# The input of a decoder's last feed-forward layer: normalisation and quantisation of three pairs of batches moved into the cross attention before it, square roots from the bits, and a quantiser in 16 bits

## The chip, the cores and the metric

The kernel runs on one core of a Trainium2 chip. A core has a TensorE (PE, with its weight loads, PEld), a VectorE (DVE), a ScalarE (ACT), a GpSimd (POOL) and a SyncE (SP), each of which works through a queue of its own in order. The metric is the device time of one execution in microseconds. Times at a place in the run are counted from the start of the profiled span.

## The reference

A decoder of three layers, each of self attention, cross attention and a feed-forward network (FFN), over 8 batches of 112 tokens with 256 values, and a context of 375 tokens with 128 values per batch. Every sublayer takes the layer-normalised `x` and is added to `x`. The change is at the end:

```python
x = x + _L3_xattn_ref(_layernorm(x, axis=-1), ctx_512, ...)   # 16 heads of 16, softmax over 375 keys
x = x + _L3_ffn_ref(_layernorm(x, axis=-1), gate_w, up_w, down_w, s_in, s_in_down)

def fake_quant_nvfp4(x, global_scale):
    xb = x.reshape(sh[:-1] + (sh[-1] // 16, 16))             # blocks of 16
    amax = jnp.max(jnp.abs(xb), axis=-1, keepdims=True)
    sc = jnp.clip(amax / 6.0 * global_scale, 0.0, 448.0)
    sc8 = sc.astype(jnp.float8_e4m3fn).astype(jnp.float32)   # scale of a block in 8 bits
    dq = sc8 / global_scale
    a = jnp.clip(jnp.abs(xb) / where(dq == 0, 1, dq), 0.0, 6.0)
    return sign(xb) * round_to(a, [0, .5, 1, 1.5, 2, 3, 4, 6]) * dq

hidden = silu(q(x) @ q(gate_w).T) * (q(x) @ q(up_w).T)       # 1024 hidden values
return q(hidden) @ q(down_w).T
```

All three weights, the input and the hidden values go through the quantiser `q`.

## The kernel before

`decoder` calls the twelve sublayers one after the other. Within most of them the inner loops stand in a `manual_schedule` region: there PE, DVE and ACT get their instructions in the order in which the code issues them. Outside such regions a scheduler decides the order on each engine from what is ready, so that the start of a sublayer can run within the end of the one before.

The names that the change touches:

- `rsqrt` (lines 410 to 422) takes variances to reciprocal roots: on DVE `va = var + eps`; on ACT a Sqrt (L415); on DVE a reciprocal (L416) and one Newton step of four operations (L418 to L421). It is called from `stats`, and this from `normalise` and `ln_T`, 35 times in the run, mostly on [112, 4] values. [...]the Sqrt takes a table load before it, and the next exponential, gelu or silu another.
- `cross` (from line 1088) is the cross attention of two layers. For each batch `b` and each group `c` of four heads it runs one step of this order: `turn` 0 and 1 (PE transposes the exponentials of one head in three pieces, DVE or ACT copies them out as `xeT`: even heads on DVE, odd ones on ACT), `key` of the next batch (c = 0, 2), `summed` (c = 1) or `divide` (c = 3) of the batch before, `turn` 2, `score` of the next step (four products into PSUM), `turn` 3, `exponent` of the next step (four maxima `xnm` on DVE, L1165; four exponentials `xe` on ACT, L1169), `value` of the next batch (PE, then the copy `xv` on DVE, L1136; c < 3), the `result` of the batch before (c = 3: projection, then the addition to `x`), and `attend` (24 products). The buffers in PSUM: `tr` two, `sc` four, `mm` and `av` one each. After the last step come the sums, a widening on POOL (`xrw`), the division (`xoT`) and the projection of the last batch.
- `quantise` (from line 1968) is the quantiser on DVE: block maxima by one reduction with absolute values (L1985), a chain on one value per block that rounds the scale to 8 bits and takes its reciprocal (L1987 to L2001), and seven operations on all values (L2004 to L2011): product with the reciprocal, clipping, exponent bits, a scaled power of two, its addition and subtraction (which rounds), and the product with the scale. All but the output are 32-bit.
- `l3_weights` quantises the three weights under the second layer's FFN, in halves of 1024 values, and transposes them.
- `l3_ffn` (from line 2060) normalises `x`, quantises it in two halves of 1024 values (four batches each), transposes each half on PE (`xqT`), and then goes over four pairs of batches: gate and up products `gu`, Silu `sg` on ACT, the product `hid` on DVE (L2104, from PSUM), `quantise` of 2048 values, transposes, a copy on ACT, the products `y` and the addition to `x` (L2121). It has no `manual_schedule`.
- `store` sends `x` out.

Of the kernel before, what the change touches and what calls it, by code (L numbers as in the profile page):

```python
# [22 lines left out]
BF16 = mybir.dt.bfloat16  # L23
AF = mybir.ActivationFunctionType
# [89 lines left out]
def _weights(inp):  # L114
# [135 lines left out]
    raw = [_fm(f("gate_w")), _fm(f("up_w")), _fm(f("down_w"))]  # L250
# [102 lines left out]
class _Kernel:  # L353
# [56 lines left out]
    def rsqrt(self, var, rows, n):  # L410

        nc, small = self.nc, self.small
        va, sd, rs, t = (self.t(small, [P, 24], tag)[:rows, :n] for tag in ("va", "sd", "rs", "nt"))
        nc.vector.tensor_scalar(va, var, EPS, None, ALU.add)
        nc.scalar.activation(sd, va, AF.Sqrt)  # L415
        nc.vector.reciprocal(rs, sd)  # L416

        nc.vector.tensor_tensor(t, rs, rs, ALU.mult)  # L418
        nc.vector.tensor_tensor(t, t, va, ALU.mult)
        nc.vector.tensor_scalar(t, t, -0.5, 1.5, ALU.mult, ALU.add)  # L420
        nc.vector.tensor_tensor(rs, rs, t, ALU.mult)  # L421
        return rs
# [666 lines left out]
    def cross(self, name, cT, qsrc, wq, wk, wv, wo, hd, scale, finish, ctx, bq=None, bk=None, bv=None):  # L1089
# [14 lines left out]
        nc, tc = self.nc, self.tc  # L1104
        acts = ctx.enter_context(tc.tile_pool(name=f"{name}_q", bufs=1))
# [135 lines left out]
        with tc.manual_schedule(engines={ET.PE, ET.DVE, ET.Activation}):  # L1241
            score(0, 0)
            exponent(0, 0)
            for n, (b, c) in enumerate(steps):
                turn(b, c, 0)
                turn(b, c, 1)
# [12 lines left out]
                if c < 3 and b + 1 < NB:  # L1259
                    value(b + 1, c)  # L1260
# [10 lines left out]
            if dense:  # L1271
                summed(NB - 1)
            divide(NB - 1)
            result(NB - 1)

# [683 lines left out]
    def l3_xattn(self):  # L1959
        w = self.w  # L1960
        with ExitStack() as ctx:
            self.cross(
                "l3x", self.ctxT, self.ln_T, w("l3x_wq", 2), w("l3x_wk"), w("l3x_wv"), w("l3x_wo", 4), 16, 0.25,
                self.add_to_x, ctx,
            )
        w.done("l3x_wo")

    def quantise(self, pool, src, dst, rows, n, gs, amax=None):
# [3 lines left out]
        nb = n // 16  # L1972

        def blocks(a):
            return a.rearrange("p (k e) -> p k e", e=16)

        def bc(a):
            return a[:, :, None].to_broadcast([rows, nb, 16])

        def sm(tag):  # L1980
            return self.t(pool, [P, nb], f"q{tag}{nb}")[:rows]

        if amax is None:
            amax = sm("m")
            nc.vector.tensor_reduce(amax, blocks(src), AX.X, ALU.max, apply_absolute_value=True)  # L1985
        sc, st, z = sm("s"), sm("t"), sm("z")
        nc.vector.tensor_scalar(sc, amax, 1.0 / 6.0, gs, ALU.mult, ALU.mult)  # L1987
        nc.vector.tensor_scalar(sc, sc, 448.0, None, ALU.min)

# [7 lines left out]
        nc.vector.tensor_tensor(sc, sc, st, ALU.subtract)  # L1997
        nc.vector.scalar_tensor_tensor(z, sc, 0.0, sc, ALU.is_equal, ALU.add)
        nc.vector.reciprocal(z, z)

        nc.vector.tensor_scalar(z, z, gs, 1.0 + 2.0**-23, ALU.mult, ALU.mult)  # L2001
        a = self.t(pool, [P, n], f"qa{n}")[:rows]
        m = self.t(pool, [P, n], f"qm{n}")[:rows]
        nc.vector.tensor_tensor(blocks(a), blocks(src), bc(z), ALU.mult)  # L2004
        nc.vector.tensor_scalar(a, a, 6.0, -6.0, ALU.min, ALU.max)

        nc.vector.tensor_scalar(m.bitcast(I32), a.bitcast(I32), 0x7F800000, None, ALU.bitwise_and)
        nc.vector.tensor_scalar(m, m, 1.0, 0.5 * big, ALU.max, ALU.mult)
        nc.vector.tensor_tensor(a, a, m, ALU.add)
        nc.vector.tensor_tensor(a, a, m, ALU.subtract)  # L2010
        nc.vector.tensor_tensor(blocks(dst), blocks(a), bc(sc), ALU.mult)  # L2011
# [146 lines left out]
```

## Time and profile before

| | us |
|---|---|
| median of three runs | 2435.77 (2435.06 to 2436.54) |
| the profiled execution | 2432.16 |
| its span | 2430.4 |
| PE busy | 2138.1 (88%) |
| DVE busy | 1434.3 (59%) |
| ACT busy | 826.8 (34%) |
| POOL busy | 215.8 (9%) |

One execution was profiled, and every duration below is from it. The execution's own time is 1.8 us above its span. A row of the profile names a line of the kernel, an engine and an operation, what is written and read (buffer numbers left out), and the shapes (partitions x elements, type). A row of the timeline starts with the time in the span and the busy time, and has in brackets how long the engine was idle before it and what ended that. Busy times are averages over stages that have different limits, so the table by stage matters more than the shares of the span.

### The profile page before, as it was taken

The page shows a single profiled execution, that of the slowest core. Times are in us where ns is not written, and L with a number is a line of the kernel's source. Part 1 is how long each engine was busy: PE and PEld are TensorE (multiplying, and loading weights), DVE is VectorE, ACT ScalarE, POOL GpSimd, SP SyncE. Part 2 cuts the span into 40 slices and gives each one's busy share as a digit, 9 for nine tenths or more (in the row PEclk, how much of TensorE's full clock was granted, in tenths as well). Part 3 has the DMA queues.
Part 4 walks back from the last instruction along what each step waited for, and adds up shares of the span by engine and source line. Part 5 has one row for each costly group of instructions (what it writes and reads, how often), then busy time and mean ns, then how long its engine had stood idle before and what let it go on. Part 6 is the DMA issues. An engine that isn't in the chain of part 4 may idle for free.

```text
span 2430.4 us, 43101 instructions
## 1 busy us (share of the span) xinstructions
PE 2138.1 (88%) x17032; PEld 1268.6 (52%) x17032; DVE 1434.3 (59%) x3810; ACT 826.8 (34%) x2220; POOL 215.8 (9%) x415
## 2 busy tenths in 40 slices
PE   6999999889899899899988859899999999899842
PEld 3444444455556566546555536466555556556622
DVE  4555556565446567553877547767740223667698
ACT  2333334453312356430111213467321111346521
POOL 0111111000011100000222331100000000100000
PEclk9999999999999999999999979999999999899966
DMA  4000000000100000100001011000111100000000
GB/s 185 2 2 2 2 20 35 29 18 18 52 1 15 18 1 2 36 26 18 35 18 35 18 28 52 17 2 19 53 35 62 41 1 1 1 1 2 2 1 15
DMA packets 10729, 55.93 MB, mean 23 GB/s; under 512 B 1833, under 2 KB 3625, under 8 KB 5792
## 3 DMA queue, kind: packets, MB, share of 16 engines
q1 hardware_dynamic: 8304, 44.57, 5.1%
q0 software_dynamic: 2080, 7.07, 0.9%
q8 instruction: 135, 2.21, 0.4%
q10 hardware_dynamic: 144, 1.54, 0.2%
q14 instruction: 66, 0.54, 0.1%
HBM read 52.23 MB, written 0.92 MB: 22 GB/s over the span
## 4 chain that ended last, share of the span: by engine, by line
PE 66%; DVE 22%; issue 5%; ACT 4%; DMA 2%; POOL 1%; DVEq 0%; ACTq 0%; POOLq 0%
PE mm L407 31%; PE tr L1178 6%; PE gu L407 6%; PE g L640 6%; PE sc L407 4%; PE av L1194 3%; PE tr L407 1%; DVE rot L1487 1%; PE av L777 1%; ACT sg L651 1%; PE av L407 1%; ACT th L662 1%; PE s L407 1%; DVE hT L666 1%; DMA cx<-in_ctx 1%
## 5 line engine op out<-in xcount | busy, mean ns | idle before, releaser
L640 PE MATMUL g<-w,hT 128*32 128x256 f32 x3552 | 237.4, 384 | 26.0 <-DVE hT L666 24.6
L1178 PEld LDWEIGHTS tr<-cst,xe 112*125 112x125 f32 x1152 | 151.5, 188 | 96.7 <-issue 37.0
L1165 DVE TENSOR_REDUCE xnm<-sc 112x1 f32<-112x375 f32 x384 | 184.3, 540 | 29.5 <-PE sc L407 28.9
L1178 PE MATMUL tr<-cst,xe 112*125 112x112 f32 x1152 | 193.1, 289 | 8.6 <-DVE xeT L1186 3.5
L407 PE MATMUL mm<-xnT,w 128*128 128x448 f32 x432 | 183.0, 559 | 19.7 <-DVE qT L1490 4.5
L407 PE MATMUL mm<-hT,w 128*128 128x448 f32 x512 | 193.0, 539 | 0.0
L640 PEld LDWEIGHTS g<-w,hT 128*32 128x32 f32 x3552 | 95.7, 109 | 167.5 <-DVE hT L666 124.6
L407 PEld LDWEIGHTS mm<-hT,w 128*128 128x128 f32 x512 | 97.1, 190 | 94.4 <-issue 94.4
L1186 DVE COPY xeT<-tr 125x336 f32<-125x336 f32 x192 | 97.3, 507 | 70.4 <-PE tr L1178 63.0
L618 PE MATMUL g<-xw,cst 128*32 128x256 f32 x1792 | 138.7, 379 | 0.0
L1184 ACT COPY xeT<-tr 125x336 f32<-125x336 f32 x192 | 85.0, 443 | 155.8 <-PE tr L1178 155.8
L407 PE MATMUL mm<-w,hT 128*112 128x256 f32 x576 | 132.6, 389 | 0.0
L407 PEld LDWEIGHTS mm<-xnT,w 128*128 128x128 f32 x432 | 77.8, 193 | 102.8 <-issue 52.6
L1169 ACT ACTIVATE xe<-sc,xnm 112x375 f32<-112x375 f32 x256 | 126.2, 581 | 9.5 <-DVE xnm L1165 9.2
L407 PE MATMUL mm<-w,oT 128*112 128x256 f32 x416 | 105.8, 405 | 24.0 <-DVE oT L1667 15.2
L407 PE MATMUL gu<-xnT,w 128*128 128x448 f32 x320 | 124.4, 544 | 1.7 <-DVE hT L1332 1.2
L407 PEld LDWEIGHTS mm<-w,hT 128*112 128x112 f32 x576 | 103.7, 182 | 27.5 <-issue 4.8
L651 ACT ACTIVATE sg<-g 128x192 f32<-128x192 f32 x224 | 73.9, 330 | 105.4 <-PE g L640 94.1
L662 ACT ACTIVATE th<-cell 128x64 f32<-128x64 f32 x224 | 57.5, 257 | 147.2 <-DVE cell L660 147.1
L407 PEld LDWEIGHTS mm<-w,oT 128*112 128x112 f32 x416 | 73.9, 186 | 54.1 <-DVE oT L1667 16.3
L664 DVE TENSOR_TENSOR h<-sg,th 128x64 f32<-128x64 f32 x224 | 50.4, 225 | 84.8 <-ACT th L662 84.8
L2046 DVE COPY wq<-tr 128x256 bf16<-128x256 bf16 (+1 forms) x12 | 4.6, 420 | 157.5 <-PE tr L2045 157.5
(398 smaller groups left out, 3673.3 us busy)
## 6 DMA issues: line engine op xcount, KB each, us to landing
w<-in_w SPq DMA_DIRECT2D x33, 1024.0 KB, 4.9
raw<-in_wq POOLq DMA_DIRECT2D x3, 1024.0 KB, 5.3
w<-in_w SPq DMA_DIRECT2D x3, 896.0 KB, 6.4
wi<-in_wint POOLq DMA_DIRECT2D x3, 768.0 KB, 5.6
w<-in_w SPq DMA_DIRECT2D x2, 768.0 KB, 4.2
ctxT<-in_ctxT ACTq DMA_DIRECT2D x1, 1500.0 KB, 8.3
cx<-in_ctx POOLq DMA_DIRECT2D x1, 1500.0 KB, 22.5
w<-in_w SPq DMA_DIRECT2D x2, 512.0 KB, 3.5
```

The lines of the kernel that those rows point to most:

```text
L407: self.nc.tensor.matmul(out, lhsT, rhs, start=i == 0, stop=i == len(pairs) - 1)
L618: nc.tensor.matmul(g[32 * j : 32 * j + 32, :], pick[:, t % 16, :], xw[:, l, t // 16, 256 * j : 256 * j + 256], start=True, stop=t == 0, sk ...
L640: nc.tensor.matmul(g[32 * j : 32 * j + 32, :], hT[l][:, c, :], whh[l][:, c, 256 * j : 256 * j + 256], start=False, stop=c == 1, skip_group ...
L651: nc.scalar.activation(sg[:, :192], g[:, :192], AF.Sigmoid)
L662: nc.scalar.activation(th, cell[l], AF.Tanh)
L664: nc.vector.tensor_tensor(h, og, th, ALU.mult)
L1165: nc.vector.tensor_reduce(nm, sc, AX.X, ALU.max, negate=True)
L1169: nc.scalar.activation(e, sc, AF.Exp, bias=nm)
L1178: nc.tensor.transpose(tp[:CH, i * S : (i + 1) * S], e[:, i * CH : (i + 1) * CH], self.ident[:S, :S])
L1184: nc.scalar.copy(eT, src)
L1186: nc.vector.tensor_copy(eT, src)
L1194: nc.tensor.matmul(avs[b][32 * j : 32 * j + 32, c * S : (c + 1) * S], values[b % 2][:CH, i, 4 * c + j, :], eTs[b, c, j][:, i, :], start=i ...
```

## The change

It has four parts.

1. `rsqrt` becomes ten operations on DVE, without ACT: a first guess from the bits of the float (shift right by one, subtract from a constant), one step of a tuned polynomial, one Newton step. `rsqrt_steps` yields within them.
2. `quantise` becomes a generator that yields after every few operations. Blocks are laid out in strides (element `e` of block `k` at `e * k_count + k`) and not side by side, so that a scale is spread over contiguous values; the weights are permuted on the host to match. The block maxima are taken of absolute values that ACT wrote (`mag`), by four maxima of halves on DVE (`block_max`); the weights keep the reduction. The quotient is cut to its upper 16 bits with the lowest bit set, and clipping, exponent bits, rounding and the last product are done in bf16.
3. The input of the last FFN goes by pairs of batches (512 values), each a generator `l3f_input` of 17 steps. `cross` calls `meanwhile(n, ps)` at places in its order; a call runs one step of the first pair whose batches are done. In the cross attention of the third layer that gives three pairs; the fourth follows in the FFN.
4. The FFN's loop gets a `manual_schedule`. While one pair is quantised the gate and up products of the next are issued between the steps, the result of a batch is issued after its half of the last product, and the additions to `x` come one pair later.

```diff
     def rsqrt(self, var, rows, n):
+        *_, rs = self.rsqrt_steps(var, rows, n)
+        return rs
+    def rsqrt_steps(self, var, rows, n):
-        nc.vector.tensor_scalar(va, var, EPS, None, ALU.add)
-        nc.scalar.activation(sd, va, AF.Sqrt)
-        nc.vector.reciprocal(rs, sd)
-        nc.vector.tensor_tensor(t, rs, rs, ALU.mult)
-        nc.vector.tensor_tensor(t, t, va, ALU.mult)
-        nc.vector.tensor_scalar(t, t, -0.5, 1.5, ALU.mult, ALU.add)
-        nc.vector.tensor_tensor(rs, rs, t, ALU.mult)
+        vec.tensor_scalar(va, var, EPS, None, ALU.add)
+        vec.tensor_scalar(r0.bitcast(I32), va.bitcast(I32), 1, None, ALU.logical_shift_right)
+        vec.tensor_scalar(r0.bitcast(I32), r0.bitcast(I32), -1.0, float(0x5F300000), ALU.mult, ALU.add)
+        yield
+        root = 0.446405130**0.5
+        vec.scalar_tensor_tensor(w, r0, root, va, ALU.mult, ALU.mult)
+        vec.tensor_tensor(w, w, r0, ALU.mult)
+        vec.scalar_tensor_tensor(p, w, -1.38883461 / root, w, ALU.add, ALU.mult)
+        yield
+        vec.scalar_tensor_tensor(p, p, 1.94247540, r0, ALU.add, ALU.mult)
+        vec.scalar_tensor_tensor(w, p, -0.5, va, ALU.mult, ALU.mult)
+        vec.tensor_tensor(w, w, p, ALU.mult)
+        vec.scalar_tensor_tensor(rs, w, 1.5, p, ALU.add, ALU.mult)
+        yield rs
...
     # cross
             for n, (b, c) in enumerate(steps):
                 turn(b, c, 0)
+                meanwhile(b - 1, ps)
                 turn(b, c, 1)
...
                     exponent(*steps[n + 1])
-                if c < 3 and b + 1 < NB:
-                    value(b + 1, c)
+                if c < 3:
+                    meanwhile(b - 1, ps)
+                    if b + 1 < NB:
+                        value(b + 1, c)
...
+            for _ in range(4):
+                meanwhile(NB - 1, ps)
             divide(NB - 1)
+            for _ in range(6):
+                meanwhile(NB - 1, ps)
             result(NB - 1)
+            for _ in range(6):
+                meanwhile(NB - 1, ps)
...
+    def l3f_inputs(self, n, ps):
+        self.l3f_ps = ps
+        while self.pairs and self.pairs[0][0] + 2 <= n:
+            if next(self.pairs[0][1], None) is not None:
+                return True
+            self.pairs.pop(0)
+        return False
+    def l3f_input(self, pool, b0):
+        for j in range(2):
+            nc.vector.bn_stats(st[:, j, :], self.x[:S, b0 + j, :])
+            nc.vector.bn_aggr(mv[:, j, :], st[:, j, :])
+            yield 1
+        for rs in self.rsqrt_steps(mv[:, :2, 1], S, 2):
+            if rs is None:
+                yield 1
+        for j in range(2):
+            nc.vector.tensor_scalar(xn in strides of 16, x, mv[:, j, 0:1], rs[:, j : j + 1], ALU.subtract, ALU.mult)
+        yield 1
+        nc.scalar.activation(mag, flat[0], AF.Abs)
+        yield 1
+        for _ in self.quantise(pool, *flat, S, 512, D, self.v("l3f_s_in")[:S], mag=mag):
+            yield 1
+        (four transposes of the pair into tr)
+        nc.scalar.copy(self.xqT[:, :, b0 * S : (b0 + 2) * S], tp)
+        yield 1
+    def block_max(self, pool, src, rows, n, row):
+        while e > 1:
+            e //= 2
+            self.nc.vector.tensor_tensor(o, a[:, :, :e, :], a[:, :, e : 2 * e, :], ALU.max)
+            a = o
...
     # quantise, on all values
+        nc.vector.tensor_tensor(wide(a), wide(src), bc(z), ALU.mult)
+        yield True
+        high = a.bitcast(I16).rearrange("p (n two) -> p n two", two=2)[:, :, 1]
+        nc.vector.tensor_scalar(b.bitcast(I16), high, 1, None, ALU.bitwise_or)
+        yield True
+        nc.vector.tensor_scalar(b, b, 6.0, -6.0, ALU.min, ALU.max)
+        nc.vector.tensor_scalar(m.bitcast(I16), b.bitcast(I16), 0x7F80, None, ALU.bitwise_and)
+        nc.vector.tensor_scalar(m, m, 1.0, 96.0, ALU.max, ALU.mult)
+        yield True
+        nc.vector.tensor_tensor(b, b, m, ALU.add)
+        nc.vector.tensor_tensor(b, b, m, ALU.subtract)
+        yield True
+        for at in range(0, n, min(n, 1024)):
+            nc.vector.tensor_tensor(wide(dst[:, part]), wide(b[:, part]), half, ALU.mult)   # half: bf16 scales
+            yield True
...
     # l3_ffn
+            with tc.manual_schedule(engines={ET.PE, ET.DVE, ET.Activation}):
+                for _ in hidden(0):
+                    for _ in range(5):
+                        self.l3f_inputs(NB, ps)
+                while self.l3f_inputs(NB, ps):
+                    pass
+                for b0 in range(0, NB, 2):
+                    later = hidden(b0 + 2) if b0 + 2 < NB else iter(())
+                    for step, _ in enumerate(filter(None, self.quantise(pool, *flat, S, 2048, 1024, s_down[:S], mag=mag))):
+                        if step == 1 and b0 > 0:
+                            add(b0 - 2)
+                            add(b0 - 1)
+                        if step >= 2:
+                            next(later, None)
+                        if step >= 6:
+                            result(b0 + step - 6, hq[:, step - 6, :])
+                add(NB - 2)
+                add(NB - 1)
```

In the new `l3_ffn`, `hidden` issues for each half of the hidden values of a batch the products, Silu, `hid` and an Abs of `hid` on ACT, and yields; `result` issues eight transposes, the copy on ACT and the eight products of one batch; `add` is the addition to `x`. The chain on the scales is that of before, with yields in it.

## The prediction

> **What bounds the kernel now.** I read the page's 40 slices first, then the table by stage for the last 300 us, then the groups of VectorE by shape in the last stage, then the timeline of one step of the last cross attention, and last the chain that ended last around the square roots. In the slices DVE is the busiest engine only at the end, and the granted clock falls there because PE idles:
>
> ```profile
> DVE  4555556565446567553877547767740223667698
> PEclk9999999999999999999999979999999999899966
> ```
>
> The table by stage (columns: stretch, length, then busy time and count of PE, PEld, DVE, ACT, POOL, then the clock) has one batch of the cross attention, its end, and pieces of the last FFN:
>
> ```profile
> 2237.20:2256.70 19.50, 19.14 (x208) 13.36 (x208) 14.53 (x33) 12.12 (x27) 0.61 (x1) 1.00 0.01 2
> 2297.20:2306.80 9.60, 6.53 (x45) 4.37 (x44) 2.56 (x11) 1.81 (x2) 0.61 (x1) 0.65 0.01 2
> 2306.80:2336.60 29.80, 10.46 (x40) 5.42 (x41) 28.18 (x55) 6.38 (x9) 0.00 (x0) 0.60 0.00 0
> 2361.30:2382.50 21.20, 8.02 (x40) 5.38 (x40) 20.87 (x24) 3.09 (x4) 0.00 (x0) 0.67 0.00 1
> 2419.10:2424.50 5.40, 4.52 (x32) 4.04 (x32) 0.96 (x3) 1.71 (x2) 0.00 (x0) 0.64 0.00 0
> ```
>
> The cross attention is PE's (19.14 of 19.5 us) with DVE free for 5.0 us in a batch; the FFN is DVE's (20.87 of 21.2). From the last addition of the cross attention (ends at 2306.8) to the last addition of the FFN it takes 117.7 us. Its groups:
>
> ```profile
> L2104 DVE SCALAR_TENSOR_TENSOR hid<-gu,sc,sg 112x512 f32<-112x512 f32 x16 | 11.9, 747 | 0.1
> L2004 DVE TENSOR_TENSOR qa<-hid,qz 112x2048 f32<-112x2048 f32 x4 | 9.2, 2292 | 0.1
> L1985 DVE TENSOR_REDUCE qm<-hid 112x128 f32<-112x2048 f32 x4 | 9.1, 2280 | 0.0
> L2007 DVE TENSOR_SCALAR qm<-qa 112x2048 int32<-112x2048 int32 x4 | 4.9, 1222 | 0.1
> L2004 DVE TENSOR_TENSOR qa<-xn,qz 112x1024 f32<-112x1024 f32 x2 | 2.4, 1224 | 0.1
> L1996 DVE TENSOR_TENSOR qs<-qs,qt 112x128 f32<-112x128 f32 x4 | 1.2, 292 | 0.1
> ```
>
> A two-input operation in 32 bits takes 2.29 us for 2048 elements, 1.22 for 1024 and 0.29 for 128, so 0.16 us and 1.04 ns an element; a one-input one runs at half that slope. Successors start 0.03 us later. A `hid` step, which reads PSUM, overlaps both neighbours: it adds 0.54 us (an operation at 2348.43, `hid` between, the next at 2350.23, against 1.26 without).
>
> **The change, part by part. 1. The quantiser of 2048 values (four times).** The block maximum turns from one reduction (2.31) into four maxima over 1024, 512, 256 and 128 elements: 1.25 + 0.72 + 0.45 + 0.32 = 2.75. The scale chain on 128 columns stays at 3.4 (2402.00 to 2405.39). The product stays at 2.32. After it the old operations cost 3 x 1.25 + 3 x 2.32 = 10.7; the new ones are an OR on every second 16-bit half, three one-input operations on bf16, two two-input ones, and two products of 1024. No DVE row of before is 16-bit throughout with its operands in SBUF. The upper bound is the 32-bit row of the same kind (1.22 and 2.29; for the OR with its step of two 2.29). The lower bound is what the Trainium skill states, "VectorE: DVE Perf Modes", section on the perf-mode tier table: for 2048 bf16 elements in SBUF 693 ns with one input and 1224 ns with two. Its 32-bit figures (1227 and 2293 ns) are this trace's rows, so I take it: 3 x 0.72 + 2 x 1.25 + 2 x 0.72 = 6.1. For the OR I take the 32-bit AND (L2007), 1.25. Sum 2.75 + 3.4 + 2.32 + 1.25 + 6.1 = 15.8 per pair (18.8 with the old operations). All at the upper bounds the pair would cost 5.9 more, four pairs 23.6.
>
> **2. The FFN from the last addition on.** Each pair of inputs (512 values) is 17 steps with 11.0 us of DVE: statistics 1.3, root 2.0 (ten small operations of 0.17 + 0.03), normalisation 0.9, maxima 1.25, scale chain 2.0, elementwise 3.5; beside it an Abs on ACT (0.6, estimated from the 0.69 of the Silu of one shape) and four transposes with a copy on ACT. Three pairs leave the FFN, but DVE's new order puts five groups of operations of the third after the last addition: 3.5. Then DVE waits: PE's order has that pair's transposes (0.6) before the first gate and up products (2.0), and Silu (0.7) follows: 3.3. First `hid` 0.65. The fourth pair 11.0, with three more `hid` (1.6) in it; its maxima wait 1.4, since its Abs stands on ACT behind the Abs of the second `hid`; 0.3 more before the first quantiser. That is 21.8. Then 4 x 15.8 = 63.3, twelve `hid` 6.5, six additions of 0.39 (2.3), 0.6 of waits for Silu behind Abs. The end gets longer, 6.7 against 5.4: the order is now written out, so PE does transposes, waits for the copy, multiplies, and only then transposes the other batch (2 x (1.0 + 0.95 + 1.45) less the 0.7 by which the first half starts early, and the addition). Sum 101.2 against 117.7: **-16.5**.
>
> **3. What the steps cost in the cross attention.** Batches 3 to 7 take 34 steps, 22 us of DVE into 5 x 5 us of idle time. But the idle time is not where the steps are:
>
> ```profile
> 2251.77 1.91 DVE L1165 TENSOR_REDUCE xnm<-sc 112x1 f32<-112x375 f32 x4 [0.37 <-PE sc L407]
> 2253.60 0.42 DVE L1136 COPY xv<-mm 125x256 f32<-125x256 f32 x1
> 2254.09 0.51 DVE L1186 COPY xeT<-tr 125x336 f32<-125x336 f32 x1
> 2254.75 0.57 PE L1221 MATMUL tr<-cst,xrw 112*128 112x112 f32 x4 [0.36 <-DVE xeT L1186]
> ```
>
> Maxima, value copy and first copy of the transposed scores follow without a gap, and PE waits for the last of them or is within 0.15 us of it (key product at 2249.73, `xv` done at 2249.53). The second call of each step is put between maxima and value copy, so there each step delays PE by its length less 0.13 of overlap and 0.13 of slack: twelve such DVE steps (0.42 to 0.92 long, 6.85 in all) 3.7, two Abs on ACT 0.5, and the transposes of pair two, whose buffer waits for a copy behind the exponentials, 1.0: 5.2. The first call falls between the first and third transposed copy, where 0.8 to 1.1 us are free; only root with normalisation (2 x 0.5), the maxima that wait for Abs behind the exponentials (1.0 and 0.9), and the transposes of pair one (1.0) stand out: 3.9. Together **+9.1**. Bounds: 0, if the next steps' slack takes it up, and 25, if all 22 us and PE's and ACT's share add up. I take the walk along the queue, as both ends ignore it.
>
> In the end of the stage four steps stand before the last division: DVE is free at 2300.0, statistics, root and normalisation take 3.6, so the division runs at 2303.6 instead of 2301.89: **+1.7**. The next six steps (3.3) lie under the last projection (3.75), so they cost nothing.
>
> **4. The roots.** 34 other sites lose the ACT step and gain four DVE operations: six at 0.2 and a 0.24 round trip (1.46) become ten (2.0). Where the root waited for nothing it costs 0.55; five such sites are on the chain (14.6, 1158, 1311.8, 1319.9, 1723.8): +2.8. Where it waited for a table it gains:
>
> ```profile
> 1301.37 1.28 ACT L415
> 1302.66 0.21 ACT sd L415
> ```
>
> Here and at 1489.8 and 2120.4 the path from variance to root was 2.76, 3.00 and 2.11: -1.9. At 522.4, 1257.2 and 1264.7 an exponential waits for the table to be loaded back, 3.1 in all, less 1.6 for added operations in that queue: -1.5. Elsewhere the roots lie in busy stretches of DVE, where two copies that overtook them give back what four operations of 0.1 cost: -0.4. Sum **-1.0**. The skill's rule would promise more: "ScalarE: Activation LUTs", section on what ACT_TABLE_LOAD costs, puts a switch of tables at 2.66 us with its drain, and 46 of 75 loads go. But the trace has the root 1.29 us after its load begins, without a second drain, and only about 7 us of loads on the chain; by the rule's price these would be 14, and the sum 7 better. I stay with the rows. Bounds -5 and +4.
>
> **5. The weights of the last FFN**, quantised under the second layer's FFN, get shorter on DVE, but PE is busy there 40.0 of 40 us; only at 1780 to 1787 does DVE's queue hold PE: **-0.5**. The reordered weights come in the same DMAs; SP's and POOL's queues stay as they were.
>
> Sum: -16.5 + 9.1 + 1.7 - 1.0 - 0.5 = **-7.2**. The profiled execution took 2432.2 (span 2430.4), so 2425.0 for its like; the median of the runs is 3.6 higher, so 2428.6. About 0.2% (4.9 us) can be told from no change here.
>
> **Rivals.** (a) The steps are hidden in the cross attention: DVE's 5 us per batch speak for it, the gapless row of maxima, value copy and transposed copy against it. The sum is then -16.3: 2419.5. Chance 0.14. (b) DVE becomes the bound of the cross attention: a batch has 14.5 us of DVE and would get 4.6 more of 19.5, and each late value copy makes the key product, the next scores and the next maxima late, in a ring. If all 25 us of inserted work land on it, the sum is +8.7, 2444.5. It decides once the stage grows by more than 16.3 instead of 9.1, two thirds of what is inserted. Chance 0.13 (0.03 of it within 0.2%). (c) The 16-bit forms run at 32-bit rates, so that the change doesn't do what it says: +23.6, 2452; the page that fits all other rows speaks against it. Chance 0.03.
>
> **How the numbers follow.** My case has 0.70, with 2422 to 2435 for it: 0.50 of it below 2430.9, 0.20 within 0.2%. Faster 0.50 + 0.14 = 0.64; same 0.20 + 0.03 = 0.23; slower 0.10 + 0.03 = 0.13. The range reaches to (a) and half the way from no change to (b): 2418 to 2440.
>
> **What would show it.** Right: 112x2048 bf16 operations at 0.69 and 1.22; a batch of the cross attention near 21.3 us from batch 3 on, 19.5 before; the last division about 1.7 later behind its operand; a wait of about 3 us before the first `hid`; 101 us from the last addition of the cross attention to the end of the FFN; 29 table loads. Wrong: batches that stay at 19.5, or reach 24; a PE that waits for `xv` in them for more than 0.5 us per step; bf16 operations at 1.2 and 2.3.

## The result, and the profile after

The changed kernel takes 2422.25 us (median of 14 runs, 2417.90 to 2431.99) against 2435.41 (14 runs, 2427.23 to 2443.62): a ratio of 0.9951, 95% interval [0.9936, 0.9966], which is 11.9 us less [8.3, 15.6]. The forecast was 7.2 less. Its direction held, and 2422.25 lies in its range, but 7.2 lies outside the interval: the size was too small by 4.7. The profiled execution of the changed kernel, 2417.9 us, is the shortest of its 14, so whole spans are not compared below. Lengths of stages are: the last FFN, for one, takes 105.25 to 105.28 us in the three kernels in which its code and order are those of after. (The decoder has four layers, counted from 0; the "third layer" whose cross attention takes the steps is layer 3, the last.)

The page of after, two of the 40 slices' rows:

```profile
DVE  4655656565545567553888457767740223668777
...
PEclk9999999899999999999999979999999999899956
```

As before, DVE is the busiest only at the end, and there the clock falls: the last but one slice has 0.5 where it had 0.6.

The table by stage of after has the columns of the one in the prediction (stretch, length, busy time and count of PE, PEld, DVE, ACT, POOL, then the clock). One batch of the cross attention, from one addition to `x` to the next; the last FFN up to the first quantiser's product; and its end:

```profile
2254.59:2274.87 20.28, 19.48 (x218) 13.56 (x207) 17.19 (x49) 12.75 (x29) 0.62 (x1) 1.00 0.01 2
...
2305.02:2334.82 29.80, 11.83 (x32) 5.68 (x33) 21.19 (x62) 8.49 (x13) 0.00 (x0) 0.60 0.00 0
...
2402.63:2410.29 7.66, 5.04 (x29) 4.08 (x26) 0.97 (x2) 1.81 (x2) 0.00 (x0) 0.50 0.00 0
```

The batch has 2.7 us more of DVE than the batch of before and is 0.8 longer; PE is busy for all but 0.8 us of it (0.4 before). In the FFN DVE is idle for 8.6 us in the first stretch, before the first pair, and for all but 1 us of the last one. In these two, and in the waits between pairs, the prediction's sum for the FFN goes wrong. The groups of VectorE in the FFN by shape (busy, mean ns of one, idle before and its releaser):

```profile
L2208 DVE SCALAR_TENSOR_TENSOR hid<-gu,sc,sg 112x512 f32<-112x512 f32 x16 | 11.9, 745 | 5.7 <-ACT sg L2207 5.3
...
L2105 DVE TENSOR_SCALAR qb<-qa 112x2048 int16<-112x2048 int16 x4 | 4.9, 1220 | 0.0
L2112 DVE TENSOR_TENSOR qb<-qb,qp 112x2048 bf16<-112x2048 bf16 x4 | 4.9, 1217 | 0.0
...
L2225 DVE SCALAR_TENSOR_TENSOR x<-y,sc,x 112x256 f32<-112x256 f32 x8 | 3.9, 482 | 8.6 <-PE y L410 8.6
L2109 DVE TENSOR_SCALAR qp<-qb 112x2048 int16<-112x2048 int16 x4 | 2.8, 695 | 0.1
```

The 16-bit operations run at the durations that were taken for them (0.69 and 1.22 us; the OR with its step of two 1.22). From its start to its first quantiser of 2048 values the FFN takes 23.6 us where it took 29.8, the four quantisers with what lies between them 74.0 and not 82.5, the rest 7.7 and not 5.4. Moving three pairs out shortens the first of these by 6 us only: the rest of the third pair, a wait of 5.3 us and the whole fourth pair still stand there. The stages, in us, each between the ends of additions to `x`:

| | before | after | difference | predicted |
|---|---|---|---|---|
| cross attention, the five batches with steps | 97.06 | 103.67 | +6.6 | +9.1 |
| its end | 9.03 | 10.35 | +1.3 | +1.7 |
| last FFN | 117.72 | 105.27 | -12.4 | -16.5 |
| sum of these | | | -4.5 | -5.7 |

So a sum of -4.5 where -5.7 was expected, and the measured 11.9. The rest, over 7 us, lies elsewhere: in the square roots, which the prediction gave 1.0, in the weights (0.5), or in the scatter of the executions. The theories for the experiments: A, the roots carry some 9 us; B, they carry 1, as predicted, and single executions scatter.

### The profile page after: what moved, and what is told of

Read it like the earlier page. It is cut to its first block, busy times and chain, and to the rows that moved or that the text cites. A ratio compares the mean times of both kernels' runs of the same rounds, so it can differ in the third digit from the quotient of the medians.

```text
span 2416.1 us, 43268 instructions
## 1 busy us (share of the span) xinstructions
PE 2146.0 (89%) x17032; PEld 1272.2 (53%) x17032; DVE 1439.4 (60%) x4056; ACT 774.5 (32%) x2161; POOL 216.9 (9%) x415
## 4 chain that ended last, share of the span: by engine, by line
PE 66%; DVE 21%; issue 5%; ACT 4%; DMA 2%; POOL 1%; DVEq 0%; ACTq 0%; POOLq 0%
PE mm L410 31%; PE gu L410 6%; PE g L656 6%; PE tr L1197 6%; PE sc L410 4%; PE av L1213 2%; PE tr L410 2%; DVE xnm L1184 1%; DVE rot L1515 1%; ACT sg L667 1%; PE av L793 1%; PE av L410 1%; ACT th L678 1%; DVE hT L682 1%; PE g L634 1%
## 5 line engine op out<-in xcount | busy, mean ns | idle before, releaser
L1188 ACT ACTIVATE xe<-sc,xnm 112x375 f32<-112x375 f32 x256 | 126.4, 583 | 11.7 <-DVE xnm L1184 11.6
```

Of the source, the lines that this page charges most:

```text
L1188: nc.scalar.activation(e, sc, AF.Exp, bias=nm)
```

## Experiments

Times are medians; ratios are to runs of before on the same chip and have 95% intervals. "The batches" is the growth of the five batches of the cross attention over the 97.06 us of before, "FFN" the length of the last FFN, both from the profile of the run. "Mean" is the difference of the mean spans with 1.96 standard errors, from the spread of the runs, and is what two changed kernels are compared by. They did not all run on the same chip, and the mean of before lies between 2432.6 and 2435.5 us on the chips, so a difference of means across chips can be off by up to 3 us. e1_roots to e4_here share one chip, e5_first to e8_both one, e9_gap and e10_ahead one, e12_order and e11_best one; after ran apart from them. Where it matters, the difference of each kernel's gain over its own before stands beside it ("by own before").

| kernel | time | ratio to before | batches | FFN |
|---|---|---|---|---|
| e1_roots | 2430.37 | 0.9988 [0.9974, 1.0003] | 0.0 | 119.4 |
| e2_noload | 2422.46 | 0.9947 [0.9927, 0.9966] | 0.0 | 118.4 |
| e3_sqrt | 2426.79 | 0.9970 [0.9955, 0.9986] | 5.7 | 105.3 |
| e4_here | 2440.62 | 1.0021 [1.0008, 1.0034] | (see there) | 123.5 |
| e5_first | 2430.48 | 0.9993 [0.9978, 1.0009] | 0.6 | 116.9 |
| e6_32bit | 2438.45 | 1.0029 [1.0013, 1.0045] | 7.4 | 122.3 |
| e7_early | 2421.64 | 0.9947 [0.9927, 0.9968] | 6.6 | 99.9 |
| e8_both | 2413.73 | 0.9921 [0.9901, 0.9941] | 6.6 | 95.7 |
| e9_gap | 2419.36 | 0.9943 [0.9922, 0.9965] | 10.5 | 97.4 |
| e10_ahead | 2412.65 | 0.9914 [0.9889, 0.9939] | 4.2 | 97.0 |
| e12_order | 2421.19 | 0.9944 [0.9924, 0.9964] | 2.4 | 105.3 |
| e11_best | 2412.21 | 0.9907 [0.9893, 0.9922] | 2.4 | 95.9 |

In after (6.6) and in the kernels e6_32bit to e9_gap the batches hold one dip of the clock, 3.4 us long; e3_sqrt has the same steps without one, so there it costs 0.9. In e9_gap the dip lies elsewhere, in the last of the five.

**e1_roots: the roots alone.**

```diff
 # before, and in rsqrt:
-        nc.scalar.activation(sd, va, AF.Sqrt)
-        nc.vector.reciprocal(rs, sd)
-        (the four operations of the Newton step)
+        *_, rs = self.rsqrt_steps(var, rows, n)
+        return rs
```

> The kernel before with the bit roots alone (ten DVE operations in place of the ACT Sqrt and six DVE operations; no other part of the change). Theory A (the profile after runs 10 us ahead of the profile before when the steps begin, at about 2170 us, and the roots alone are the cause): 9 to 10 us faster than before, 2425.9, and the last feed-forward stage as before (117.7 us from the last addition of the cross attention to its own last addition). Theory B (my sum, roots -1.0): 2434.4, within the noise of before; the 10 us at 2170 would then be scatter between single executions. In between, the rest is scatter. Table loads 29 by both.

Measured: 2430.37, ratio 0.9988, 2.9 us less [6.3 less, 0.7 more]. A's 9 to 10 is outside the interval, and B's 1.0 is inside it. In this trace the FFN is 1.7 longer than before's: its root, which waited for no table before, brings 0.6 of it (the prediction had 0.55 for such a site), and the products at the end, at a lower clock, 0.8.

**e2_noload: the 46 loads of the roots gone, ACT still on the way.** The root itself is left out. The trace of before has 75 table loads of 1.28 us, 29 of them ahead of a Sqrt (L415); this kernel and e1_roots have 29 in all.

```diff
-        nc.scalar.activation(sd, va, AF.Sqrt)
+        nc.scalar.copy(sd, va)
```

> The kernel before with a copy on ACT in place of the Sqrt; it leaves the root itself out. The way over ACT and the six DVE operations stay, the 46 table loads go. If the gain of the roots comes from the loads alone, this gains at least what the bit roots gain, and more by what the ten operations cost on the chain: by my rows 0.55 us at five places and 1.6 in the layers with a busy DVE queue, some 4 us: 13 us faster than before where the bit roots give 9. If the gain comes from taking ACT's queue out of the path (waits of the small Sqrt behind other work on ACT), this gains clearly less than the bit roots: under 5 us. If theory B holds: 3 to 5 us faster (the loads' 3.4 us, without the added operations).

Measured: 12.9 us less [8.3, 17.8] than before (10.9 +- 2.2 by the means), and 7.9 (+-3.0, means) less than e1_roots. So the loads are what was worth removing, and more than the prediction's rows gave them. The kernel with the longer chain of operations in the Sqrt's place hands most of it back; how much of that is the chain itself and how much the clock, the table below parts.

**e3_sqrt: the change without its roots.**

```diff
 # after, with the Sqrt on ACT, reciprocal and Newton step of before in rsqrt;
 # the steps in the cross attention and the fourth pair keep the bit roots
```

> The kernel after with the old roots over ACT at all places but the steps of the last feed-forward's input. Theory A: it gives back 9 to 10 us of the 13: 2432, 3 faster than before. Theory B: 1 us slower than after, 2423. There may be something on top: the fourth pair and the steps keep the bit roots, so 35 minus 1 roots and some 46 loads come back, none in the last stage.

Measured: 7.3 us less than before [3.4, 11.0], where the prediction's other terms (-16.5 + 9.1 + 1.7 - 0.5) come to 6.2, and 4.6 more than after (by the ratios; 3.7 +- 3.5 by the means). So the best estimates for the roots are 3 to 5 us in either setting. By the means they are 3.0 +- 2.7 and 3.7 +- 3.5 (the second 5.7 +- 4.3 by own before): 9 is outside the first, and 1 is not excluded.

Where do A's 10 us at 2170 us come from, then? The last addition before the steps begin ends at 2200.70 us in the trace of before and at 2191.00 in that of after. The table by stage up to there, of before and then of after:

```profile
0.00:2200.70 2200.70, 1995.78 (x15792) 1171.04 (x15792) 1252.61 (x3505) 745.93 (x2061) 212.09 (x409) 0.97 0.07 25
```

```profile
0.00:2191.00 2191.00, 1994.54 (x15792) 1170.43 (x15792) 1263.30 (x3645) 683.23 (x1982) 213.24 (x409) 0.97 0.07 25
```

PE does the same work, ACT has 62.7 us less (45 loads of 1.28 up to there are 58), DVE 10.7 more, and the clock is the same: each trace has dips of 129.7 us in all at half the clock, which is 64.9 us of clock lost. So the 9.7 us are saved work at equal clock. It is rather the roots' than the weights': the trace of e3_sqrt, with the new weights and the old roots, is 0.3 us later than before at this addition once its lost clock (59.7) is taken off. In the trace of e1_roots the dips up to the same addition (at 2202.50) lose 73.4 us: it is 1.8 us later than before, and 6.7 earlier once the lost clock is taken off. The two profiles of before and after happen to have the same dips; the runs as a whole do not. In every trace here the dips are multiples of 3.4 us at 0.5, but for one cut off by the end of the span, and all changes of the clock in one trace lie on one grid of 3.41 us (to 0.004), whose place against the start of the span differs from trace to trace. The Trainium skill, "TensorE: Matmul & The Clock Gate", section "What's actually happening", has the rule behind it: a window of 3.4 us that runs freely and halves the clock after an idle window. Its length, the one half and the free running agree with the traces; that the place of the grid decides which waits of PE become a dip would explain the scatter, but no run here shows that. Over 105 runs of before, span and mean clock have a correlation of -0.86, and a microsecond of lost clock goes with 0.70 us of span.

The mean span and clock of each kernel part the two. This is an account and not a cause, since clock that PE loses while DVE sets the pace, as in the last stage, costs little:

| | span x clock | span x (1 - clock) |
|---|---|---|
| e1_roots less before | -8.2 +- 1.3 | +5.2 +- 3.1 |
| after less e3_sqrt | -9.5 +- 1.5 | +5.8 +- 4.0 |
| e2_noload less before | -13.5 +- 2.0 | +2.6 +- 3.2 |
| e1_roots less e2_noload | +5.3 +- 2.2 | +2.6 +- 4.0 |

Twice the same: by this account the roots bring 8 to 9.5 us, and 5 to 6 go again with more lost clock. If a microsecond of lost clock costs 0.70 and not 1, the roots bring 6.7 to 7.8 at equal clock. Theory A had the size of that, the runs show the difference. Of the 7.9 between e1_roots and e2_noload, 5.3 are the longer chain and 2.6, not told from nothing, are clock. Why kernels with the bit roots lose more clock is left open.

A place that the prediction took for covered, in the trace of before and then of e1_roots:

```profile
575.02 0.16 DVE L414 TENSOR_SCALAR va<-mv 112x4 f32<-112x4 f32 x1
...
575.39 1.28 ACT L415 ACT_TABLE_LOAD   x1
576.97 0.68 DVE L857 TENSOR_SCALAR qT<-mm,vec 128x448 f32<-128x448 f32 x1 [1.79 <-PE mm L407]
...
578.57 1.38 DVE L445 TENSOR_SCALAR xn<-x,mv,rs 112x256 f32<-112x256 f32 x4
```

```profile
574.00 0.16 DVE L420 TENSOR_SCALAR va<-mv 112x4 f32<-112x4 f32 x1
...
575.78 0.16 DVE L434 SCALAR_TENSOR_TENSOR rs<-rw,rp 112x4 f32<-112x4 f32 x1
575.98 1.38 DVE L458 TENSOR_SCALAR xn<-x,mv,rs 112x256 f32<-112x256 f32 x4
```

From `va` to the normalisation it takes 3.55 us before and 1.98 with the bit roots. The load stands on ACT behind a copy (`xnT`, to 575.37), and by the time the root is there, DVE has the copy `qT` in front of the reciprocal; the ten operations run in the 1.8 us in which DVE waited for PE.

**e4_here: no steps in the cross attention.**

```diff
-                self.add_to_x, ctx, meanwhile=self.l3f_inputs,
+                self.add_to_x, ctx,
...
+                while self.pairs[0][0] == 0:
+                    self.l3f_inputs(NB, ps)
                 for _ in hidden(0):
```

> The kernel after without any step in the cross attention: all of the four pairs' normalisation and quantisation stand in the last feed-forward (the first pair before the first products, the others between the quantiser steps as after). The cross attention should be as before (19.5 us a batch, its growth of 6.2 and the later end of 2.0 gone) and the feed-forward longer by three pairs of 11 us of DVE less the 3.5 that it has already: 29.5 us, from 105.3 to about 135. Sum: +29.5 - 8.2 = 21 slower than after, 2443. If the steps in the cross attention cost it more than the profile's single execution showed (my 9.1 + 1.7), 2441; if they cost nothing there, 2451.

Measured: 2440.62, 15.7 +- 3.2 (means; 17.7 +- 4.0 by own before) slower than after, where 21 was expected. The FFN is 18.2 us longer and not 29.5: the scheduler, which orders what stands outside the written order, put the first pair's operations into the cross attention, between 2174.6 and 2218.5 us, from the time when its batches were ready. One interval between additions there is 23.58 instead of 19.5 (it has a dip of 3.4 us as well). So this kernel has one pair there without any plan, and two pairs of 11.0 less 3.5 moved, 18.5: the term for a pair is confirmed, with two pairs and not three.

**e5_first: only the first call of a step.**

```diff
                 if c < 3:
-                    meanwhile(b - 1, ps)
                     if b + 1 < NB:
                         value(b + 1, c)
```

> The kernel after with only the first call of a step (between the first and the second turn); the second call, between the maxima and the value copy, is gone, so that batches 3 to 7 take 20 steps and not 34, and 14 to 15 steps come later. If the second call is what delays PE (my 5.2 of 9.1), the growth of the cross attention up to its last batch falls from the 5 to 6 us that three kernels with steps showed to about 2.5; if the first call or ACT's and PE's own share does it, it falls only with the number of steps, to about 3.5; if it is the number of matmuls and the copies of the pairs' transposes, which come later too, to under 1. The steps that are left (some 9.7 us of DVE) go into the feed-forward: 6 us slower than after, 2429.

Measured: the batches are as before: 19.49, 19.52, 19.50, 19.48, and 0.6 more in the last. Twenty steps between the first and second turn cost 0.6 us, where the prediction had 3.9 for them. With the second call come fifteen more steps, and the other 5.1 us. The key products in the groups of PE in the cross attention, of after and then of this kernel (idle before, and its releaser):

```profile
L410 PE MATMUL mm<-ctxT,w 128*128 128x375 f32 x20 | 8.4, 499 | 0.7 <-DVE xv L1155 0.7
```

```profile
L410 PE MATMUL mm<-ctxT,w 128*128 128x375 f32 x20 | 8.1, 486 | 0.0
```

The wait for the value copy `xv` is there with the second call and gone without it. It is a part of the 5.1: with 0.4 in another row of after the waits put down to `xv` are 1.1. In all PE idles for 3.8 us of the five batches in before, 4.2 here, and 6.4 in e3_sqrt, which has after's steps and no dip; the rest of the growth is in PE's busy time. The FFN gets 11.6 us longer and the end of the cross attention 1.0 longer than after's, and the kernel is 7.0 +- 3.4 slower than after (9.9 +- 4.5 by own before): the second call is worth its price.

**e6_32bit: the new order, 32-bit values.**

```diff
-        b, m = (self.t(pool, [P, n], f"q{i}{n}", BF16)[:rows] for i in "bp")
+        b, m = a, self.t(pool, [P, n], f"qp{n}")[:rows]
...
-        high = a.bitcast(I16).rearrange("p (n two) -> p n two", two=2)[:, :, 1]
-        nc.vector.tensor_scalar(b.bitcast(I16), high, 1, None, ALU.bitwise_or)
...
 # scales, mask and constants in 32 bits likewise
```

> The kernel after with the quantiser's values in 32 bits: no OR, and clipping, exponent bits, rounding and the last product in f32 instead of bf16; order, layout and maxima as after. By the rows of after (112x2048: 0.69 and 1.22 in bf16, 1.22 and 2.28 in f32): -1.22 for the OR, 3 x 0.53, 2 x 1.06 and 2 x 0.54 more, +3.6 a pair, 14.4 in the four pairs, and 0.9 for the fourth input, on the path; about 1 in the cross attention. 16 us slower than after, 2438. If the 16-bit operations weren't on the path of the feed-forward (PE or ACT sets it), under 8.

Measured: 2438.45, 16.2 over after's median (16.6 +- 3.9 by the means, 19.5 +- 4.9 by own before); its FFN is 17.0 longer in the trace. The bf16 forms, and not only the new order, carry the FFN's gain of 12.4; with 32-bit values the whole change is slower than before by 0.29% [0.13, 0.45]. One of its rows, from the groups of VectorE (1.22 in bf16):

```profile
L2111 DVE TENSOR_TENSOR qa<-qa,qp 112x2048 f32<-112x2048 f32 x4 | 9.2, 2291 | 0.1
```

**e7_early and e8_both: the start and the end of the FFN.** What the wait before the first `hid` is made of, in the timeline of after:

```profile
2309.09 0.53 ACT L2043 COPY xqT<-tr 128x448 bf16<-128x448 bf16 x1 [8.12 <-PE tr L2040]
...
2311.69 1.28 ACT L2207 ACT_TABLE_LOAD   x1 [2.08 <-PE gu L410]
2312.99 0.69 ACT L2207 ACTIVATE sg<-gu,sc 112x512 f32<-112x512 f32 x1
2313.71 0.75 DVE L2208 SCALAR_TENSOR_TENSOR hid<-gu,sc,sg 112x512 f32<-112x512 f32 x1 [5.27 <-ACT sg L2207]
```

The prediction counted transposes, products and Silu, 3.3. The 1.28 of Silu's table load and the 0.53 of the copy `xqT` are missing from it. And the end, from the first batch's products on:

```profile
2404.06 1.96 PE L410 MATMUL y<-wq,hqT 128*112 128x256 bf16 x8 [1.05 <-ACT hqT L2219]
...
2405.81 0.95 PE L2217 MATMUL tr<-ident,hq 112*128 112x112 bf16 x8
...
2409.81 0.48 DVE L2225 SCALAR_TENSOR_TENSOR x<-y,sc,x 112x256 f32<-112x256 f32 x1 [3.27 <-PE y L410]
```

PE waits for the copy and does the second batch's transposes only after the first's products, at half the clock. The edits (the second kernel has the first's too):

```diff
 # e7_early: in cross, the last six calls go
-            for _ in range(6):
-                meanwhile(NB - 1, ps)
...
 # and in the FFN a yield ahead of the first hid, with six steps there
+                        if (b0, j, i) == (0, 0, 0):
+                            yield
...
-                for _ in hidden(0):
-                    for _ in range(5):
+                for n, _ in enumerate(hidden(0)):
+                    for _ in range(5 if n else 6):
...
 # e8_both: transposes and copy of both batches, then both products
-                            result(b0 + step - 6, hq[:, step - 6, :])
+                            hTs = (hTs if step == 7 else []) + [turned(hq[:, step - 6, :])]
+                    for j in range(2):
+                        result(b0 + j, hTs[j])
```

> The kernel after with the first gate and up products and their Silu issued ahead of the last six steps of the third pair, which move behind them out of the end of the cross attention. The wait of 5.3 us of DVE before the first `hid` should fall to about 2, as the rest of the third pair (3.5 us of DVE) lies under the products and the Silu: 3 us faster than after in the feed-forward, 2419.5. If what delays the first `hid` is the fetch of the stage (Silu's table, the copy of `xqT`) and not the order, 0.

> As the kernel with the early products, and besides, in each pair both batches' transposes and copies are issued ahead of the two `y` products, so that PE doesn't wait for a copy between them. The stretch from the last product of the quantiser to the last addition, 7.7 us in the profile of after, should fall to about 6; between pairs the second addition's wait for `y` (0.6) goes. 2 us faster than with the early products alone, 2417.5. If the copy on ACT isn't what holds PE there (the clock of 0.5 in the last stretch makes products slow), 0 to 1.

Measured, first kernel: the FFN takes 99.9 us, 5.4 less, more than the 3 expected. The first `hid` now follows without a wait, and the four products took 1.02 us and not 2.0, since the clock was full (its timeline):

```profile
2313.05 1.02 PE L410 MATMUL gu<-wq,xqT 128*112 128x512 bf16 x4 [0.51 <-DVE x L500]
...
2316.33 0.74 DVE L2208 SCALAR_TENSOR_TENSOR hid<-gu,sc,sg 112x512 f32<-112x512 f32 x1
```

Its time, 3.4 +- 4.9 (means) under after, cannot be told from after's. Second kernel: the FFN takes 95.7, the end 5.6 and not 7.7, and the time is 9.8 +- 4.6 under after (means; 6.9 +- 5.4 by own before): a version better than both kernels. In its timeline of the end both batches' products are one row, and PE's wait for a copy is 0.30 once:

```profile
2397.71 3.66 PE L410 MATMUL y<-wq,hqT 128*112 128x256 bf16 x16 [0.30 <-ACT hqT L2219]
```

**e9_gap, e10_ahead, e12_order, e11_best: the place of the second call.** The edits, over e8_both for the first, over the one before it for the second, over after for the third, and over e8_both for the fourth, which has the third's edit:

```diff
 # e9_gap: one more call, and none ahead of the last division
                 attend(b, c)
+                if c == 3:
+                    meanwhile(b, ps)
...
-            for _ in range(4):
-                meanwhile(NB - 1, ps)
             divide(NB - 1)
 # e10_ahead, e12_order, e11_best: the second call ahead of the maxima
                 turn(b, c, 3)
+                if c < 3:
+                    meanwhile(b - 1, ps)
                 if n + 1 < len(steps):
                     exponent(*steps[n + 1])
                 if c < 3:
-                    meanwhile(b - 1, ps)
                     if b + 1 < NB:
                         value(b + 1, c)
```

> The kernel with early products and both batches' transposes, and two places changed: one more call of a step per batch, after the addition to x of the batch before (c = 3), where DVE waits 0.80 us for PE in the trace with first calls only; and no steps ahead of the last division. The added call should cost the batches nothing (they stay at 19.8 to 20.5 us), the last division comes 1.75 us earlier, and the third pair is done sooner (4 steps left after the last addition, not 6): 2 to 3 us faster, 2411. If the gap behind the addition isn't free (PE's next transposes wait for the step), each of the six added steps costs up to 0.5 and the two effects cancel: 2413 to 2414.

> As the kernel before it in this list, and the second call of each step stands ahead of the maxima and not behind them, where DVE waits 0.37 us for the scores. If the delay of PE comes from what stands between the maxima and the value copy, the growth of a batch falls from 0.3 to 1.0 to 0 to 0.4, in all 2 to 4 us: 2408. If a step ahead of the maxima delays them, and through the exponentials the next transposes, as much as it delayed the value copy, 0.

> The kernel after with one edit: the second call of a step stands ahead of the four maxima and not between them and the value copy. The number of steps in the cross attention stays. If the place is what delays PE, the growth of the cross attention, 5.9 us in the trace of after from the fourth addition to its last batch's, falls to 2 and the kernel gets 4 us faster than after: 2418.5. If the number of steps does it, it stays at 6: 2422.

> The early products, both batches' transposes, and the second call ahead of the maxima, with the four steps ahead of the last division and without the call behind the addition. The trace with that call grew by 3.9 us more in the batches for seven steps; without it and with the better place the cross attention should grow by 2 us and end 1.75 later: 95.7 us of feed-forward and 4 us less of cross attention than with the transposes alone, 2410. If the gain of the last run but this came from the missing steps ahead of the division, 2413.

Measured: e9_gap has 3.9 us more in the batches than e8_both for five steps more (40 and not 35 within them), with a dip in both, so the gap behind the addition isn't free; the end is 1.3 shorter (9.03). The second of its two theories was nearer, and its time of 2419.36 is worse than either gave. e10_ahead gains 6.3 us of growth over it (4.2 for 10.5), a part of it because it has no dip there, and 5.8 +- 4.1 in the means. e12_order isolates the place: 2.4 of growth for 5.7 without the dip, with the FFN at 105.27 as in after. Its time, 1.1 under after's median, is not to be told from after (2.2 +- 5.6 less by the means); the 4 us of the expectation are 3.3 in the trace and stay unproved in the time. The first second call of batch 3, with statistics, in after and then in e12_order (neither is in a dip):

```profile
2193.96 1.91 DVE L1184 TENSOR_REDUCE xnm<-sc 112x1 f32<-112x375 f32 x4 [0.37 <-PE sc L410]
...
2195.79 0.42 DVE L2017 BATCH_NORM_STATS2 st<-x 112x6 f32<-112x256 f32 x1
...
2196.34 0.39 DVE L1155 COPY xv<-mm 125x256 f32<-125x256 f32 x1
...
2196.79 0.95 PE L410 MATMUL mm<-cst,xoT 128*112 128x4 f32 x8 [0.22 <-DVE xv L1155]
```

```profile
2201.55 0.42 DVE L2017 BATCH_NORM_STATS2 st<-x 112x6 f32<-112x256 f32 x1
...
2202.10 1.89 DVE L1184 TENSOR_REDUCE xnm<-sc 112x1 f32<-112x375 f32 x4
...
2203.91 0.42 DVE L1155 COPY xv<-mm 125x256 f32<-125x256 f32 x1
...
2204.45 0.88 PE L410 MATMUL mm<-cst,xoT 128*112 128x4 f32 x8
```

From the maxima to the value copy it takes 2.38 us and then 1.81. Ahead of the maxima DVE waits 0.37 for the scores, as in the prediction's row, and most of the step (0.55) lies in that wait: over the five batches the waits of the maxima for the scores are 4.1 us in e3_sqrt and 0.4 in e12_order. PE's wait for `xv` is gone, and its idle time is 4.3 us, near before's. e11_best, with all that paid, is at 2412.21, ratio 0.9907 [0.9893, 0.9922], the lowest here: 11.8 +- 2.9 under after by the means (11.5 +- 3.9 by own before). In its trace the FFN is 9.4 shorter than after's, by e8_both's edits, and the batches are 4.2 shorter, with 0.9 of a dip in it; against e8_both itself it is 2.0 +- 4.1 lower, which is not clear of noise.

## Why the prediction was right, and where it wasn't

1. *The quantiser in 16 bits* was right: 0.69 and 1.22 us as taken, the OR at the value of the 32-bit row. Rival (c) is gone, and e6_32bit shows its price: 16 us, where the prediction had 23.6 for all forms and the OR at the upper bound.
2. *The FFN*, -16.5, was too good by 4.1. Three terms of the sum were mis-sized. The wait before the first `hid`: 5.27 and not 3.3, since Silu's table load and the copy were left out; the first quantiser starts 23.6 after the addition, not 21.8. The four quantisers: 74.0 and not 72.7, since the second addition of a pair waits 0.63 for `y`, three times, where no wait was foreseen. The end: 7.7 and not 6.7, since the products ran at half the clock (1.96 for 1.45, which was the mean of a row that in before ran in part at the full clock).
3. *The steps in the cross attention*, +9.1, were too dear by 3.4. Rivals (a), no growth, and (b), all 25 us, are gone with it: a batch takes 20.6 on average without the dip, where 21.3 was the sign and 19.5 or 24 the contrary. The total of the second call was right: 5.2 expected, and 5.1 is what is left of 5.7 without the first call's 0.6; its three parts were not measured one by one. (The steps in these batches are 35, not 34.) The first call's 3.9 failed: the walk let root, maxima and transposes stand out of a gap of 0.8 to 1.1 us, and e5_first shows that nothing behind the gap waited for them. The mechanism that decided is the one named, what stands between the maxima and the value copy: with the same number of steps, e12_order takes 3.3 of the 5.1 away by the place alone. The 1.8 that are left there go with the number of steps or with causes that were not parted.
4. *The end of the stage*: +1.7 expected, +1.3 measured.
5. *The roots*, -1.0, are the step that made the sum too small. Their best estimates are 3 to 5. The price of the loads is the term that was mis-sized: it was taken at six places on the chain, 6.6 by the prediction's rows (5.0 as it stands, with three sites already less the 1.6 of their added operations), and e2_noload brings 12.9 for all. So the six places were not all: one more, at 575 us, is shown, the others were not looked up. The added operations were given 6.0 with that 1.6; they cost 5.3 +- 2.2 by the account above, which is near, and 7.9 with the clock that goes along. The sum had no term for that clock. The Trainium skill's rule ("ScalarE: Activation LUTs", section "What ACT_TABLE_LOAD costs"), which would have made the sum 7 better, comes out nearer the 12.9 of the loads, but not for its reason: the root follows 1.29 us after the start of its load in the trace, without a second drain.
6. *The weights*, -0.5: not tried by itself, and too small to be seen. Nor were the layout in strides, the four maxima in place of one reduction, or the FFN's written order without the rest.

With the measured terms, -12.4 + 6.6 + 1.3 and -3 to -5 for the roots, the sum is -7.5 to -9.5; the interval of the measurement begins at -8.3, and what is left to its middle, 2.4 to 4.4, has no cause shown: it lies within the noise of the measurements. That the forecast came near is in part luck: the FFN's error, +4.1, and the first call's, -3.3, undid each other.

## What to carry to other kernels

Work that is put into another stage's idle time costs by its place: on the engine it must stand where the engine already waits for the bottleneck, not between an operation and the one whose result the bottleneck needs next; 20 steps cost 0.6 us in one place, and 15 cost 5.1 in another and 1.8 in a third. When a function of ScalarE is replaced to save table loads, count the loads (12.9 us here) and the longer chain that takes its place (5.3, or 7.9 with the clock that went along) separately, over all sites. Where the granted clock dips at other places in every execution, compare many runs and the lengths of stages; before positions in two single traces are compared, the clock that each has lost up to there is to be taken off.

## What the runs showed of the hardware

The dips of the granted clock, in multiples of 3.4 us at half the clock, go with a scatter of the whole time that is larger than any term of this change: runs of before spread from 2422.35 to 2444.61 us. A change that saves work can lose half of it again with the clock (8.2 saved and 5.2 lost with the roots alone); the cause of that was not found. And written order binds only what stands in it: in e4_here operations placed behind the cross attention in the code ran within it, most of them in its fourth batch.
